# Attention over heads in a four-layer gated cross-attention stack: half-height products for the row maxima, and reciprocals by Ln, Exp and a Newton step

## The chip, the core and the metric

The kernel runs on one core of one Trainium2 chip. The metric is the device time of a whole run in microseconds; shown are the median and the ends of several runs. A profile comes from one further execution, and its span is counted from the first to the last recorded instruction.

The engines are called as the profile calls them: PE is TensorE's products, PEld its weight loads, DVE is VectorE, ACT is ScalarE, POOL is GpSimd, and SP is the queue that issues most DMAs.

## What is computed

A residual stream `x` of 2 batches x 1024 positions x 256 channels passes four layers. Each layer adds a gated cross-attention to a short context (77 rows per batch) and then a gated feed-forward block. Layers 0, 2 and 3 attend with 16 heads of 16 channels; layer 1 attends with one head over all 256 channels. Layer 2 turns queries and keys by position (rope). Layers 2 and 3 mask context rows. Cut to an attention over heads, the reference is:

```
q = heads(layernorm(x) @ Wq + bq)        # 16 heads, 16 channels each
k = heads(ctx @ Wk + bk);  v = heads(ctx @ Wv + bv)
s = q k^T * scale;  s = where(mask, -big, s)
p = softmax(s);  o = p v
x = x + tanh(g) * (o @ Wo + bo)
```

The feed-forward blocks are a mixture of 8 experts with a shared one, a mixture of 16, a quantised two-layer block, and a mixture of 8 with a shared one. The change leaves them alone.

## The kernel before

Everything is float32 unless it is a mask or a piece of a maximum. The 2048 rows of `x` stay in SBUF as 16 tiles of 128 rows, in four blocks `j` of four tiles `k`. `heads_attention` (lines 390 to 634) does layers 0, 2 and 3; it is a generator whose first part (keys, values and the tables made of them) can run under the feed-forward block before it.

**Its preparation.** `kT` holds the keys with channels on partitions, in two halves `ec` of 128 channels (8 heads each). `kbd` (line 430) repeats them 8 times along the free axis, each time kept for one head's 16 partitions only by `headmask`, so that one product of 128 partitions with four such groups gives four heads' scores side by side (4 x 77 = 308 columns). `kz` and `va` are the tables for the probabilities and for the values.

**Its loop.** For each block `j` these steps follow one another in an order written out in lines 611 to 629, which runs several blocks at once:

- `norm(j)`: layernorm of the rows, transposed to `hT`; the power -0.5 is on POOL.
- `queries(j, ec)`: the projection to `qT`.
- `maxima(j, k)`: for each `ec` and each half `hf` of the eight heads, one float32 product of 308 columns on all 128 partitions (line 498), in layers 2 and 3 a bfloat16 product that adds the mask (line 504), and a VectorE reduce that takes the maximum of each head's 77 scores, negated (line 508). Each result lies in one of four PSUM tiles of the pool `mm`, which nearly all products share in turn.
- `split(j)` and `turned(j)`: the maxima are split in three bfloat16 parts and transposed to `MT`.
- `probabilities(j, ec, i)`: the scores again, now with the context on partitions, as four products on quarters of the partitions (line 546); the maxima are subtracted by a product with a selection matrix (line 553), and ScalarE takes Exp (line 561).
- `combine(j, ec)`: sums `pz` and weighted values `pa` by two groups of products (line 574). VectorE takes the reciprocal of the sums (line 579) and multiplies (line 582), which gives `atT`.
- `finish(j)`: the output projection (line 589), added to `x` with the gate `tg` (line 593).

A block's `maxima` run between the `probabilities` of the block before it; the last block has none to run there. In layers 2 and 3, `behind` starts the norm of the following feed-forward block on finished rows. The framework that builds the program may move an instruction ahead of others on its engine where its inputs allow it, so the order on an engine can differ a little from the order of the code. It also puts in the loads of ScalarE's function tables where the next function is not in the loaded set.

Of the kernel before, what the change touches and what calls it, by code (L numbers as in the profile page):

```python
# [8 lines left out]
F32 = mybir.dt.float32  # L9
# [3 lines left out]
AF = mybir.ActivationFunctionType  # L13
ALU = mybir.AluOpType
AX = mybir.AxisListType
# [3 lines left out]
P = 128  # L19
D = 256  # L20
# [3 lines left out]
TB = 512  # L24
NK = 77
# [25 lines left out]
def flamingo_kernel(  # L51
# [4 lines left out]
    V, S, G, T = nc.vector, nc.scalar, nc.gpsimd, nc.tensor  # L56

    const = ctx.enter_context(tc.tile_pool(name="const", bufs=1))
# [11 lines left out]
    def mm(name, dt=F32, cols=512):  # L70
        return psA.tile([P, cols], dt, tag="mm", name=name)
# [5 lines left out]
    xs = []  # L77
# [60 lines left out]
    ident16 = const.tile([P, P], BF16, tag="ident16", name="ident16")  # L138
# [6 lines left out]
    headmask = const.tile([P, 8], F32, tag="headmask", name="headmask")  # L145
# [7 lines left out]
    )  # L153


    parity = const.tile([P, 2], F32, tag="parity", name="parity")
    for i in range(2):
        V.tensor_reduce(parity[:, i : i + 1], headmask[:, i::2], AX.X, ALU.add)
# [24 lines left out]

    tg = const.tile([P, 8], F32, tag="tg", name="tg")
    S.activation(tg, bc[:, 16:24], AF.Tanh)


    ctxT = const.tile([P, 2, 2 * NK], F32, tag="ctxT", name="ctxT")
# [7 lines left out]
    mskp = {}  # L196
# [115 lines left out]
    def bcl(ap, n):  # L312

        return ap.unsqueeze(2).to_broadcast([ap.shape[0], ap.shape[1], n])

    def bcm(ap, n):

        return ap.unsqueeze(1).to_broadcast([ap.shape[0], n, ap.shape[1]])
# [52 lines left out]
    def value(l, w, b):  # L371

        pv = mm(f"v{l}_{b}")
        for dc in range(2):
            T.matmul(
                pv[:NK, 0:D], lhsT=ctxT[:, dc, b * NK : (b + 1) * NK], rhs=w["v"][:, dc, :],
                start=(dc == 0), stop=(dc == 1),
            )
        return pv
# [10 lines left out]
    def heads_attention(l, ahead=None, behind=None):  # L390


        scale = 1.0 if l == 2 else 1.0 / 4.0
        with ExitStack() as st:
            ap1 = st.enter_context(tc.tile_pool(name=f"at1_{l}", bufs=1))
# [8 lines left out]
            kT = ap1.tile([P, 2, 2 * NK], F32, tag="kT", name=f"kT{l}")  # L404
# [22 lines left out]
                )  # L427
            kbd, vz = [], []
            for b in range(2):
                kb = ap1.tile([P, 2, 8, NK], F32, tag=f"kbd{b}", name=f"kbd{l}_{b}")  # L430
                for ec in range(2):
                    V.tensor_tensor(
                        kb[:, ec], bcm(kT[:, ec, b * NK : (b + 1) * NK], 8), bcl(headmask, NK), ALU.mult
                    )
                kbd.append(kb)
                va = ap1.tile([NK1, NH, 2 * DH], F32, tag=f"va{b}", name=f"va{l}_{b}")
                pv = value(l, w, b)
                G.memset(va, 0.0)
                for i in range(2):
                    V.tensor_tensor(  # L440
                        va[:NK, i::2, i * DH : (i + 1) * DH],
                        pv[:NK, 0:D].rearrange("p (h d) -> p h d", d=DH)[:, i::2, :],
                        w["bv"][:NK].rearrange("p (h d) -> p h d", d=DH)[:, i::2, :], ALU.add,
                    )
                vz.append(va)
# [12 lines left out]
            ap2 = st.enter_context(tc.tile_pool(name=f"at2_{l}", bufs=2))  # L458
            ap3 = st.enter_context(tc.tile_pool(name=f"at3_{l}", bufs=3))
            ap4 = st.enter_context(tc.tile_pool(name=f"at4_{l}", bufs=4))  # L460
            hTs, qTs, MTs, pTs, atTs, nms = {}, {}, {}, {}, {}, {}
# [27 lines left out]
            def maxima(j, k):  # L489

                i = 4 * j + k
                b, sq = i // NST, i % NST
                if k == 0:
                    nms[j] = ap2.tile([P, 4, 4, 2, 2], F32, tag="nm", name=f"nm{l}_{j}")
                for ec in range(2):
                    for hf in range(2):
                        ps = mm(f"sc{l}_{i}_{ec}_{hf}")
                        T.matmul(  # L498
                            ps[:, 0 : 4 * NK], lhsT=qTs[j][:, ec, k * P : (k + 1) * P],
                            rhs=kbd[b][:, ec, 4 * hf : 4 * hf + 4, :].rearrange("p h k -> p (h k)"),  # L500
                            start=True, stop=not masked,
                        )
                        if masked:
                            T.matmul(  # L504
                                ps[:, 0 : 4 * NK], lhsT=ident16, rhs=bcm(mskp[l][0][:, sq, :], 4),
                                start=False, stop=True,
                            )
                        V.tensor_reduce(  # L508
                            nms[j][:, k, 2 * hf : 2 * hf + 2, ec, :],
                            ps[:, 0 : 4 * NK].rearrange("p (r i k) -> p r i k", i=2, k=NK), AX.X, ALU.max, negate=True,  # L510
                        )

            def split(j):
# [17 lines left out]
            def turned(j):  # L531

                sq = (4 * j) % NST
                pm = mm(f"mT{l}_{j}", BF16, 1024)
                for k in range(4):
                    T.transpose(pm[:, k * P : (k + 1) * P], madd[:, sq + k, :], ident16)
                MTs[j] = ap2.tile([P, TB], BF16, tag="MT", name=f"MT{l}_{j}")
                S.copy(MTs[j], pm[:, 0:TB])

            def probabilities(j, ec, i):  # L540

# [22 lines left out]
            def combine(j, ec):  # L564

                b = j // 2
                nk = NK1 if l == 2 else NK
                pa, pz = mm(f"av{l}_{j}_{ec}"), mm(f"as{l}_{j}_{ec}")
                for po, lhsT in (
                    (pz, lambda r, i: ones2[:, i, :]), (pa, lambda r, i: vz[b][:, 8 * ec + 2 * r + i, :]),  # L570
                ):
                    for i in range(2):
                        for r in range(4):
                            T.matmul(  # L574
                                po[32 * r : 32 * r + 32, :], lhsT=lhsT(r, i)[:nk], rhs=pTs[j, ec, i][:nk, r, :],
                                start=(i == 0), stop=(i == 1),
                            )
                rz = ap1.tile([P, TB], F32, tag="rz", name=f"rz{l}_{j}_{ec}")
                V.reciprocal(rz, pz)  # L579
                if ec == 0:  # L580
                    atTs[j] = ap2.tile([P, 2, TB], F32, tag="atT", name=f"atT{l}_{j}")
                V.tensor_tensor(atTs[j][:, ec, :], pa, rz, ALU.mult)

            def finish(j):
                for k in range(4):
                    i = 4 * j + k
                    po = mm(f"o{l}_{i}")
                    for ec in range(2):
                        T.matmul(  # L589
                            po[:, 0:D], lhsT=atTs[j][:, ec, k * P : (k + 1) * P], rhs=w["o"][:, ec, :],  # L590
                            start=(ec == 0), stop=(ec == 1),
                        )
                    V.scalar_tensor_tensor(xs[i], po[:, 0:D], tg[:, l : l + 1], xs[i], ALU.mult, ALU.add)


            def has(step, j, *rest):
# [7 lines left out]
            for k in range(4):  # L604
                maxima(0, k)
# [1231 lines left out]
```

## Time and profile before

| | us |
|---|---|
| median of 3 runs | 1559.37 |
| lowest, highest | 1556.24, 1565.51 |
| profiled execution | 1588.63 |
| its span | 1586.9 |
| mean granted TensorE clock in it | 0.925 of full |

| group in the profile before | count | mean ns | busy us |
|---|---|---|---|
| L498 product for maxima (two records each) | 384 | 439 | 125.8 |
| L504 mask product | 128 | 304 | 38.9 |
| L508 maximum | 192 | 476 | 88.7 |
| L561 Exp | 96 | 1016 | 92.7 |
| L579 reciprocal | 24 | 3356 | 80.5 |
| L582 product with it | 24 | 692 | 16.6 |
| L432 `kbd` | 12 | 952 | 11.2 |

In a group's row of the profile, the numbers after the count are busy time and the mean duration of one; after the next bar stands the time for which the engine was idle just before these instructions, and what ended most of that. In the timeline a row gives the start, the time from the first start to the last end, the engine, the line, the operation, and how many instructions of that kind are merged. Product records overlap each other, so the distance between starts says more than a record's length.

### The profile page before, as it was taken

The page shows a single profiled execution, that of the slowest core. Times are in us where ns is not written, and L with a number is a line of the kernel's source. Part 1 is how long each engine was busy: PE and PEld are TensorE (multiplying, and loading weights), DVE is VectorE, ACT ScalarE, POOL GpSimd, SP SyncE. Part 2 cuts the span into 40 slices and gives each one's busy share as a digit, 9 for nine tenths or more (in the row PEclk, how much of TensorE's full clock was granted, in tenths as well). Part 3 has the DMA queues.
Part 4 walks back from the last instruction along what each step waited for, and adds up shares of the span by engine and source line. Part 5 has one row for each costly group of instructions (what it writes and reads, how often), then busy time and mean ns, then how long its engine had stood idle before and what let it go on. Part 6 is the DMA issues. An engine that isn't in the chain of part 4 may idle for free.

```text
span 1586.9 us, 18081 instructions
## 1 busy us (share of the span) xinstructions
PE 1358.2 (86%) x6798; PEld 901.4 (57%) x6800; DVE 890.0 (56%) x2168; ACT 403.7 (25%) x676; POOL 318.0 (20%) x367
## 2 busy tenths in 40 slices
PE   6999996999999999969759996889965899985783
PEld 3453445888888888536648883434433454344562
DVE  7676676444444444565653116757789667682124
ACT  1332430333333233213101111022355222211230
POOL 3200002222212110250010104400013400005661
PEclk9999997999999999989859997989987999997897
DMA  4001005565656556320315872000000000023545
GB/s 160 4 14 49 27 1 209 177 214 180 227 174 229 178 184 220 116 70 10 112 44 193 306 291 95 27 7 1 1 27 20 1 1 28 27 80 93 168 141 176
DMA packets 48362, 169.87 MB, mean 107 GB/s; under 512 B 9039, under 2 KB 27634, under 8 KB 42258
## 3 DMA queue, kind: packets, MB, share of 16 engines
q0 software_dynamic: 15600, 88.23, 16.0%
q1 hardware_dynamic: 25664, 74.33, 13.3%
q10 hardware_dynamic: 7010, 6.15, 1.3%
q8 instruction: 54, 0.88, 0.2%
q14 instruction: 34, 0.28, 0.1%
HBM read 147.97 MB, written 20.71 MB: 106 GB/s over the span
## 4 chain that ended last, share of the span: by engine, by line
PE 31%; DVE 11%; DMA 7%; issue 3%; POOL 2%; ACT 1%; another core or an unknown queue 1%; POOLq 0%; DVEq 0%; ACTq 0%; SPq 0%
DMA wbig<-in_wbig_dram 4%; PE sc L498 4%; PE q L384 2%; PE h L1199 2%; PE as L574 2%; PE gur L1557 2%; PE sT L546 2%; PE sT L553 2%; PE eo L1212 1%; PE av L574 1%; PE hs L941 1%; PE o L589 1%; PE gus L1557 1%; DVE hmax L1390 1%; PE eo_s L1007 1%
## 5 line engine op out<-in xcount | busy, mean ns | idle before, releaser
L941 PE MATMUL hr<-xgT0s,w 128*128 128x256 f32 (+1 forms) x1536 | 300.5, 346 | 11.5 <-DVE ulr L947 11.3
L941 PEld LDWEIGHTS hr<-xgT0s,w 128*128 128x128 f32 x1536 | 246.5, 191 | 55.6 <-DVE ulr L947 25.0
L561 ACT ACTIVATE pT<-sT 78x1024 f32<-78x1024 f32 x96 | 92.7, 1016 | 230.8 <-PE sT L553 208.9
L498 PE MATMUL sc<-kbd,qT 128*128 128x308 f32 x384 | 125.8, 439 | 7.3 <-DVE qT L480 6.2
L941 PE MATMUL hs<-hT_f,w0s 128*128 128x512 f32 x256 | 117.7, 602 | 5.5 <-DVE uls L947 2.2
L947 DVE SCALAR_TENSOR_TENSOR ulr<-hr,w,ulr 128x256 f32<-128x256 f32 (+1 forms) x96 | 41.6, 434 | 130.1 <-ACT ulr L946 129.5
L508 DVE TENSOR_REDUCE nm<-sc 128x4 f32<-128x308 f32 x192 | 88.7, 476 | 45.1 <-PE sc L504 33.4
L579 DVE RECIPROCAL rz<-as 128x512 f32<-128x512 f32 x24 | 80.5, 3356 | 29.6 <-PE as L574 29.6
L498 PEld LDWEIGHTS sc<-kbd,qT 128*128 128x128 f32 x384 | 68.3, 197 | 44.7 <-issue 19.6
L941 PEld LDWEIGHTS hs<-hT_f,w0s 128*128 128x128 f32 x256 | 46.9, 193 | 56.6 <-issue 47.9
L946 ACT ACTIVATE ulr<-hr,w 128x256 f32<-128x256 f32 (+1 forms) x96 | 41.7, 434 | 146.2 <-PE hr L941 146.0
L1025 PE MATMUL eo<-w,hid_r 128*128 128x256 f32 x312 | 77.5, 379 | 0.0
L384 PE MATMUL q<-hT_a,aw 128*128 128x512 f32 x128 | 71.5, 692 | 7.0 <-DVE hT_a L306 4.9
L1199 PE MATMUL h<-xgTs,wbig 128*128 128x128 f32 x512 | 62.7, 283 | 5.7 <-DMA wbig<-in_wbig_dram 5.7
L1199 PEld LDWEIGHTS h<-xgTs,wbig 128*128 128x128 f32 x512 | 61.1, 198 | 9.4 <-issue 6.0
L969 POOL DMA_INDIRECT w<-in_wbig_dram,r_wr_f x24 | 23.2, 965 | 212.7 <-PE hr L941 130.9
L1557 PE MATMUL gur<-xT3s,w 128*128 128x256 f32 (+1 forms) x192 | 50.0, 414 | 14.4 <-ACT xT3s L1605 7.8
L1549 DVE TENSOR_TENSOR sg_r<-gur,sg_r 128x256 f32<-128x256 f32 (+1 forms) x24 | 9.0, 375 | 94.9 <-ACT sg_r L1548 49.4
L1025 PEld LDWEIGHTS eo<-w,hid_r 128*128 128x128 f32 x312 | 57.8, 190 | 7.6 <-issue 0.5
L946 ACT ACTIVATE ugr<-hr,w 128x256 f32<-128x256 f32 (+1 forms) x96 | 41.7, 434 | 77.9 <-PE hr L941 71.1
L1212 PE MATMUL eo<-wbig,hh 128*128 128x256 f32 x256 | 59.9, 379 | 0.0
L947 DVE SCALAR_TENSOR_TENSOR ugr<-hr,w,ugr 128x256 f32<-128x256 f32 (+1 forms) x96 | 41.5, 433 | 31.4 <-ACT ugr L946 15.4
(457 smaller groups left out, 2295.1 us busy)
## 6 DMA issues: line engine op xcount, KB each, us to landing
wbig<-in_wbig_dram SPq DMA_DIRECT2D x17, 2048.0 KB
w<-in_wbig_dram SPq DMA_DIRECT2D x24, 384.0 KB
w0s<-in_wbig_dram SPq DMA_DIRECT2D x2, 2048.0 KB
h_dram<-h_f SPq DMA_DIRECT2D x32, 128.0 KB
y<-y_dram SPq DMA_DIRECT2D x4, 1024.0 KB
eo_dram<-eo0s SPq DMA_DIRECT2D x15, 256.0 KB
x<-in_x_dram SPq DMA_DIRECT2D x4, 512.0 KB
aw<-in_aw_dram SPq DMA_DIRECT2D x2, 1024.0 KB
```

The source lines that it names most:

```text
L384: T.matmul(pq, lhsT=w[m][:, dc, ec * P : (ec + 1) * P], rhs=hT[:, dc, :], start=(dc == 0), stop=(dc == 1),)
L498: T.matmul(ps[:, 0 : 4 * NK], lhsT=qTs[j][:, ec, k * P : (k + 1) * P], rhs=kbd[b][:, ec, 4 * hf : 4 * hf + 4, :].rearrange("p h k -> p (h ...
L508: V.tensor_reduce(nms[j][:, k, 2 * hf : 2 * hf + 2, ec, :], ps[:, 0 : 4 * NK].rearrange("p (r i k) -> p r i k", i=2, k=NK), AX.X, ALU.max, ...
L561: S.activation(pT[:, 2 * a : 2 * a + 2, :], pp[a][:NK1], AF.Exp, scale=scale)
L579: V.reciprocal(rz, pz)
L941: T.matmul(both[a][:, wi, :], lhsT=w13[:, dc, wi, a, ic * P : (ic + 1) * P], rhs=rhs(dc), start=(dc == 0), stop=(dc == 1),)
L946: S.activation(uu, both[a][:, 0, :], AF.Identity, bias=bias[:, 0, a, ic : ic + 1])
L947: V.scalar_tensor_tensor(uu, both[a][:, 1, :], bias[:, 1, a, ic : ic + 1], uu, ALU.add, ALU.mult)
L1025: T.matmul(po[:, s * D : (s + 1) * D], lhsT=hid[:, ic, s * P : (s + 1) * P], rhs=w2[:, ic, :], start=(ic == 0), stop=(ic == 3),)
L1199: T.matmul(ph[:, fc // 4, (fc % 4) * C : (fc % 4 + 1) * C], lhsT=w1[:, dc, fc * P : (fc + 1) * P], rhs=xgTs[e][:, dc, :], start=(dc == 0), ...
L1212: T.matmul(po[:, 0:D], lhsT=hs[e][:, fc // 4, (fc % 4) * C : (fc % 4 + 1) * C], rhs=w2[:, fc, :], start=(fc == 0), stop=(fc == NF - 1),)
L1557: T.matmul(pa[:, s, 0:n], lhsT=w[:, s, dc, :], rhs=rhs(dc), start=(dc == 0), stop=(dc == 1))
```

## The change

Three things change in `heads_attention`, and two small tables are made for them at the start.

**The products for the maxima.** `kbd` repeats the keys 4 times instead of 8, masked by `headmask4`, which is the sum of the two halves of `headmask`: column `h` keeps head `h` on partitions 0 to 63 and head `h + 4` on partitions 64 to 127. For each `ec`, the half `hf` now multiplies only partitions `64 hf` to `64 hf + 63` of `qT` and `kbd`, again with 308 columns. Both PSUM tiles are taken first, both float32 products follow one another, and then, in a second loop, come the mask products (as before, on all partitions) and the reduces.

**The reciprocal.** ScalarE takes Ln of the sums and Exp of its negative, which gives an approximate reciprocal `r`. VectorE computes `at = pa * r`, then `pz * r`, then `(pz * r - 2) * at`. This is a Newton step with its sign turned, so `finish` multiplies by `ntg`, the negated gate. `rz` now has two buffers.

**The table.** After the copy of `MT` for block 0, one load of ScalarE's table set that holds both Ln and Exp is issued.

```diff
+    headmask4 = const.tile([P, 4], F32, tag="headmask4", name="headmask4")
+    V.tensor_tensor(headmask4, headmask[:, 0:4], headmask[:, 4:8], ALU.add)
...
+    ntg = const.tile([P, 4], F32, tag="ntg", name="ntg")
+    V.tensor_scalar(ntg, tg[:, 0:4], -1.0, None, ALU.mult)
...
-                kb = ap1.tile([P, 2, 8, NK], F32, tag=f"kbd{b}", name=f"kbd{l}_{b}")
+                kb = ap1.tile([P, 2, 4, NK], F32, tag=f"kbd{b}", name=f"kbd{l}_{b}")
...
-                        kb[:, ec], bcm(kT[:, ec, b * NK : (b + 1) * NK], 8), bcl(headmask, NK), ALU.mult
+                        kb[:, ec], bcm(kT[:, ec, b * NK : (b + 1) * NK], 4), bcl(headmask4, NK), ALU.mult
...
+                    ps = [mm(f"sc{l}_{i}_{ec}_{hf}") for hf in range(2)]
                     for hf in range(2):
-                        ps = mm(f"sc{l}_{i}_{ec}_{hf}")
+                        half = slice(64 * hf, 64 * hf + 64)
                         T.matmul(
-                            ps[:, 0 : 4 * NK], lhsT=qTs[j][:, ec, k * P : (k + 1) * P],
-                            rhs=kbd[b][:, ec, 4 * hf : 4 * hf + 4, :].rearrange("p h k -> p (h k)"),
+                            ps[hf][:, 0 : 4 * NK], lhsT=qTs[j][half, ec, k * P : (k + 1) * P],
+                            rhs=kbd[b][half, ec].rearrange("p h k -> p (h k)"),
                             start=True, stop=not masked,
                         )
+                    for hf in range(2):
                         if masked:
                             T.matmul(
-                                ps[:, 0 : 4 * NK], lhsT=ident16, rhs=bcm(mskp[l][0][:, sq, :], 4),
+                                ps[hf][:, 0 : 4 * NK], lhsT=ident16, rhs=bcm(mskp[l][0][:, sq, :], 4),
...
-                S.copy(MTs[j], pm[:, 0:TB])
+                copied = S.copy(MTs[j], pm[:, 0:TB])
+                if j == 0:
+                    with tc.issue_after(copied.ins):
+                        S.preload_act_table_set("natural_log_exp_and_others")
...
-                rz = ap1.tile([P, TB], F32, tag="rz", name=f"rz{l}_{j}_{ec}")
-                V.reciprocal(rz, pz)
+                rz = ap2.tile([P, TB], F32, tag="rz", name=f"rz{l}_{j}_{ec}")
+                S.activation(rz, pz, AF.Ln)
+                S.activation(rz, rz, AF.Exp, scale=-1.0)
...
-                V.tensor_tensor(atTs[j][:, ec, :], pa, rz, ALU.mult)
+                at = atTs[j][:, ec, :]
+                V.tensor_tensor(at, pa, rz, ALU.mult)
+                V.tensor_tensor(rz, pz, rz, ALU.mult)
+                V.scalar_tensor_tensor(at, rz, 2.0, at, ALU.subtract, ALU.mult)
...
-                    V.scalar_tensor_tensor(xs[i], po[:, 0:D], tg[:, l : l + 1], xs[i], ALU.mult, ALU.add)
+                    V.scalar_tensor_tensor(xs[i], po[:, 0:D], ntg[:, l : l + 1], xs[i], ALU.mult, ALU.add)
```

## The prediction

> **What bounds the kernel now.** First the page: its busy rows and the slices that hold the three attentions over heads (slices 1 to 4, 26 to 30 and 32 to 35 of 40).
>
> ```profile
> span 1586.9 us, 18081 instructions
> PE 1358.2 (86%) x6798; PEld 901.4 (57%) x6800; DVE 890.0 (56%) x2168; ACT 403.7 (25%) x676; POOL 318.0 (20%) x367
> PE   6999996999999999969759996889965899985783
> DVE  7676676444444444565653116757789667682124
> ```
>
> Then the stage windows of the three loops, in layers 0, 2 and 3 (columns: window, length, busy PE, PEld, DVE, ACT, POOL, granted clock, DMA).
>
> ```profile
> 60.00:119.00 59.00, 58.09 (x360) 29.16 (x362) 44.19 (x85) 20.49 (x24) 2.03 (x2) 1.00 0.03 10
> 1060.00:1123.00 63.00, 60.91 (x344) 30.54 (x344) 45.90 (x91) 13.99 (x15) 2.03 (x2) 1.00 0.00 1
> 1236.00:1347.00 111.00, 110.57 (x592) 55.39 (x592) 75.05 (x169) 30.50 (x37) 14.38 (x18) 0.98 0.03 10
> ```
>
> TensorE is occupied 97 to 100% of the loops at full clock and nothing waits long on DMA; VectorE has a quarter to a third free, ScalarE two thirds. A microsecond of TensorE work removed there is a microsecond of time, unless VectorE is late behind it. Then the groups that the change touches:
>
> ```profile
> L498 PE MATMUL sc<-kbd,qT 128*128 128x308 f32 x384 | 125.8, 439 | 7.3 <-DVE qT L480 6.2
> L508 DVE TENSOR_REDUCE nm<-sc 128x4 f32<-128x308 f32 x192 | 88.7, 476 | 45.1 <-PE sc L504 33.4
> L579 DVE RECIPROCAL rz<-as 128x512 f32<-128x512 f32 x24 | 80.5, 3356 | 29.6 <-PE as L574 29.6
> L432 DVE TENSOR_TENSOR kbd<-kT,headmask 128x616 f32<-128x616 f32 x12 | 11.2, 952 | 0.0
> ```
>
> A float32 product is two matmul records (384 for 192). Records overlap, so I price by distance between starts, from the timeline:
>
> ```profile
> 79.90 4.31 PE L498 MATMUL sc<-kbd,qT 128*128 128x308 f32 x16
> 84.04 0.38 PE L589 MATMUL o<-aw,atT 128*128 128x256 f32 x1
> 1299.09 0.30 PE L504 MATMUL sc<-madd,ident 128*128 128x308 bf16 x1
> 1299.75 0.30 PE L504 MATMUL sc<-madd,ident 128*128 128x308 bf16 x1
> ```
>
> Layer 0: eight products in 4.14 us, 0.517 each. Layers 2 and 3: 0.655 per product with its mask; so the mask is 0.655-0.517, about 0.13. A pair of half-head groups (one `i`, one `ec`) costs 1.035 without and 1.31 with masks.
>
> **The pairs.** The new operands lie on partitions 0-63 and 64-127. Whether such products run together, L546 shows; it already uses quarters of the partitions:
>
> ```profile
> 1337.81 0.67 PE L546 MATMUL sT<-qT,kz 32*78 32x512 f32 x4
> 1338.30 0.61 PE L546 MATMUL sT<-qT,kz 32*78 32x512 f32 x4
> 1338.84 0.41 PE L553 MATMUL sT<-MT,pick 128*78 128x512 bf16 x1
> ```
>
> Four first passes start together, four second passes 0.49 later, the next, full-height product 0.54 after those. A pass of 512 columns is 0.43 (L384 spaces its weight loads so), so eight passes took 1.03 us where a queue of them would take 3.41. The excess over 0.86 is 0.06 for the first weights (78 columns) and 0.1 for emptying the array where the height changes.
>
> So a new pair is 0.517. In layer 0 neighbours have one height: 1.035 becomes 0.517. In layers 2 and 3 each pair goes to half height and back for its masks: weights 0.11 (0.06 scaled to 128 columns) + 0.517 + change 0.1 + first mask weights 0.03 + masks 0.26 + change 0.1 = 1.11, a saving of 0.20. The Trainium skill speaks against this part: "TensorEngine Tiling (Array Packing)", Key Properties, says that a change of tiling mode drains TensorE. It gives no price; the row's 0.1 is used. Taken as free, 64 masked pairs would save 26 us; with it, 12.8.
>
> What of it reaches the end:
> - Layer 0, three turns of the loop. Reduces of L508 run back to back at 0.41 us (four in 1.63 at 91.56), and four PSUM tiles turn under all `mm` products. For k=0 and k=3, four tiles: 2.07 becomes 1.03, saving 1.0 each. For k=1 and 2 together, the fifth tile waits for a reduce: 4.14 becomes about 2.75, saving 1.4. 3 x 3.4 = 10.2. But k=3 meets a busy VectorE at 91.56: `as` already waited 0.91 for it; that 1.0 and some of the next goes into the wait. Kept: 8. The opening `maxima(0)` (29 to 37 us) runs at VectorE's pace: nothing.
> - Layers 2 and 3: k=0 saves 0.4, k=1,2 0.8, k=3 0.4 only where no norm of finished rows stands ahead of its reduces (one turn of three; `as` already waits 1.04, 1.05, 0.38 and 0.38 in the others). 3 x 1.2 + 0.4 = 4 each, and 1 each in the openings: 10.
>
> **Smaller `kbd`.** L432 halves to 308 elements: twelve instructions from 0.95 to about 0.55 (L425, 308 elements, 0.61). In layer 0 four of them (3.3 us) stand ahead of the copy of `hT` that TensorE awaits at 21.63: 1.5, less 0.1 for the new `headmask4`. In layer 3 they lie in the VectorE-bound stage (1206 to 1211, 4.7 us): 2.1. Layer 2 prepares them under other work: 0. Sum 3.5. If covers existed there too, 0.
>
> **The reciprocal.** Out: 3.36 on VectorE, 24 times. In: on ScalarE Ln (PSUM, 512 columns: L1205, 0.60) and Exp (SBUF: L953, 0.63); on VectorE two more operations of 0.69 (L582, L956). From sums to `atT`: before 3.36 + 0.10 + 0.69 = 4.15; after 0.60 + 0.63 + 3 x 0.69 + 0.1 for hand-overs = 3.4. Inside the loop this lies under the next products, and nothing follows but freedom: VectorE gets 24 x (3.36 - 1.38) = 47 us back, ScalarE gives 30, 1.2 per combine, out of its idle two thirds. On the path it lies twice per layer, at the last turn without maxima to cover it:
>
> ```profile
> 1353.71 3.36 DVE L579 RECIPROCAL rz<-as 128x512 f32<-128x512 f32 x1 [4.77 <-PE as L574]
> 1357.17 0.69 DVE L582 TENSOR_TENSOR atT<-av,rz 128x512 f32<-128x512 f32 x1
> 1357.92 2.24 PEld L589 LDWEIGHTS o<-aw,atT 128*128 128x128 f32 x11 [0.50 <-DVE atT L582]
> ```
>
> 6 x 0.75 = 4.5. New waits: Ln waits on ScalarE for the sums, with the next Exps behind it; these need a product of L553 that ends over 3 us later (sums done 1364.9, next Exp 1368.47), so they lose nothing. VectorE's product waits 1.3 us for Exp; queued behind it are reduces and `hT` copies that before waited 3.36 for the reciprocal. The sums' tile is held 0.60+0.63+1.38, not 3.36, so PSUM comes free earlier.
>
> **The table.** One preload per head layer behind a copy; the row of L953's loads says 1.28 us. The Trainium skill, "ScalarE: Activation LUTs", What ACT_TABLE_LOAD costs, says 2.66 with its drain. At most three: 3.8 or 8.0 us of ScalarE, which is idle there 1 us or more; the path gets 0.1 each by the row, 1.4 by the page. I take 0.3 in all. Should the loads alternate between Ln and Exp, see below. `ntg` is nothing.
>
> **Sum:** 8 + 10 + 1.4 + 2.1 + 4.5 - 0.3 = 25.7 off the profiled 1586.9 (1588.6 with its surroundings). That execution is 29 above the median; its head stages run at full clock, so the same microseconds are taken from 1559.4: **1533.7**, 1.6%.
>
> **Rivals.**
> (1) As summed, 1534; own range 1521 to 1546, as VectorE eats half of the layer 0 and masked gain, or none. Chance 0.65.
> (2) VectorE sets the pace: each burst of pairs ends in a wait for its reduce, and the maxima give a third (6). 1559.4 - 6 - 7.7 = 1546, at worst 1555. For it: `as` waits on `nm` now. Against: VectorE loses 50 us of work in these stages. Chance 0.14.
> (3) Slower: halves do not run side by side. Masked pairs then cost 1.035 + 0.6 = 1.63, 64 x 0.32 = 20 more; layer 0 nothing; minus 7.7: 1571. It decides when a pair takes over about 0.9 instead of 0.517 (26 us fall by 66 per us added). Against: L546. For: no half-height product is in this trace. Chance 0.10.
> (4) Tables alternate, two loads per combine: 48 x 1.28 = 61 us of ScalarE, most hidden, 3 us in each of six exposed chains: 1534 + 18 = 1552. Against: Tanh and Exp share one load before. Chance 0.05.
> (5) VectorE's freedom also shortens the openings and the norm waits: 1515. Chance 0.06. (The order of instructions on an engine is not the code's, e.g. `as` at 1348.24 ahead of `sT`; a new order can add a few us to any case.)
>
> **The numbers.** A measurement here tells 0.5%, 7.8 us. Faster by that: nearly all of (1) and (5), two thirds of (2): 0.80; same: the rest of (2), (4) and an edge of (3): 0.11; slower: (3): 0.09. Range 1514 to 1558: it leaves out (3) and the ends of (2), (4) and (5).
>
> **What would show it.** Products of 64 rows starting in twos, half of the loops' L498 spacing in layer 0, and about 1.1 us per masked pair; Ln before Exp with at most three new table loads; no L579; `as` waits on `nm` up by 1 to 2 us per turn. The prediction is wrong if 64-row products start one after another, if a change of height costs over 0.2, or if a table load stands at each combine.

## The result and the profile after

The changed kernel takes 1547.49 us (median of 7 runs, 1544.84 to 1552.55) where the kernel before takes 1559.72 beside it; the ratio is 0.9922, 95% interval 0.9905 to 0.9939. That is 12.2 us less (9.5 to 14.8), where 25.7 were forecast. Of the profiled execution the span is 1548.9 us.

First the page of the changed kernel: busy rows, and the slices of TensorE and VectorE.

```profile
span 1548.9 us, 18125 instructions
PE 1337.7 (86%) x6798; PEld 861.6 (56%) x6800; DVE 831.7 (54%) x2194; ACT 437.6 (28%) x727; POOL 316.0 (20%) x367
...
PE   5999987999999999969849996889977799996873
...
DVE  7565675444444444466562115755569945566214
```

VectorE lost 58 us of work (the forecast: 47 from the reciprocals and about 5 from `kbd`) and ScalarE gained 34, as worked out. The slices say little; the stage windows say more (window, length, busy PE, PEld, DVE, ACT, POOL, granted clock, DMA). The first, second and last row are the loops of layers 0, 2 and 3; the third and fourth row lie inside layer 2's loop.

```profile
55.00:110.00 55.00, 52.63 (x368) 23.41 (x364) 34.64 (x89) 23.74 (x30) 1.02 (x1) 1.00 0.03 11
1060.00:1123.00 63.00, 60.07 (x314) 22.16 (x316) 33.15 (x83) 18.14 (x22) 2.02 (x2) 0.84 0.00 1
1069.60:1080.00 10.40, 10.38 (x45) 2.61 (x46) 4.46 (x12) 1.92 (x3) 0.00 (x0) 0.52 0.00 0
1107.00:1118.00 11.00, 10.73 (x48) 2.81 (x48) 4.71 (x13) 2.16 (x4) 0.00 (x0) 0.53 0.01 1
1219.00:1330.00 111.00, 106.00 (x598) 42.48 (x600) 67.87 (x187) 38.03 (x48) 18.14 (x22) 0.97 0.03 10
```

Before, layer 2's loop ran at a granted clock of 1.00. Now it has 0.84, and the two inner rows show why: twice, for some 10 us, TensorE is busy all the time at half its clock. Busy time alone hides this; only the clock column tells.

The groups that the change touches:

```profile
L505 PE MATMUL sc<-kbd,qT 64*128 64x308 f32 x384 | 83.0, 501 | 5.7 <-DVE qT L485 3.5 <-DVE nm L516 1.1 <-ACT qT L492 1.1
L516 DVE TENSOR_REDUCE nm<-sc 128x4 f32<-128x308 f32 x192 | 81.2, 470 | 44.3 <-PE sc L512 32.6 <-PE sc L505 11.3
L597 DVE TENSOR_TENSOR atT<-av,rz 128x512 f32<-128x512 f32 x24 | 16.6, 692 | 75.1 <-PE av L586 75.1
L592 ACT ACTIVATE rz<-as 128x512 f32<-128x512 f32 x24 | 14.3, 597 | 45.7 <-PE as L586 45.6
L437 DVE TENSOR_TENSOR kbd<-kT,headmask 128x308 f32<-128x308 f32 x12 | 7.3, 629 | 0.0
L550 ACT ACT_TABLE_LOAD x3 | 3.8, 1283 | 0.1
```

The products for the maxima have 64 rows now; the tables cost three loads in all. `L597` is the product `pa * rz`: where VectorE stands idle in front of it, 75.1 us in all, it waits for the values `av`, never for the reciprocal.

The timeline of the changed kernel (start, time from first start to last end, engine, line, how many, idle time before) in layer 0 and, after the first dots, around the first wait in layer 2:

```profile
84.13 1.31 PE L505 MATMUL sc<-kbd,qT 64*128 64x308 f32 x8
...
87.38 1.92 PE L586 MATMUL as<-pT,ones 77*32 77x512 f32 x16 [1.94 <-DVE nm L516]
...
1065.89 0.79 PE L505 MATMUL sc<-kbd,qT 64*128 64x308 f32 x4
1066.54 1.38 DVE L1327 TENSOR_SCALAR h<-x,mv_f,rs_f 128x256 f32<-128x256 f32 x4 [1.20 <-POOL rs_f L1325]
...
1066.61 0.45 PE L512 MATMUL sc<-madd,ident 128*128 128x308 bf16 x2
1066.99 0.79 PE L505 MATMUL sc<-kbd,qT 64*128 64x308 f32 x4
...
1067.96 1.22 DVE L1330 TENSOR_REDUCE rmax<-h 128x4 f32<-128x1024 f32 x1
1069.10 1.62 DVE L516 TENSOR_REDUCE nm<-sc 128x4 f32<-128x308 f32 x4
1069.62 3.29 PE L586 MATMUL as<-pT,ones 78*32 78x512 f32 x16 [1.46 <-DVE nm L516]
...
1072.67 3.66 PE L586 MATMUL av<-pT,va 78*32 78x512 f32 x16
```

Eight records, two pairs, take 1.31 us in layer 0 from the first start to the last end; two products start together each time, and the later starts in that row are 0.26 apart, two of them to a pair, so 0.52 a pair. A masked pair takes 1066.99 - 1065.89 = 1.10: 0.72 to its first mask product and 0.38 from there to the next pair, where the forecast had 0.73 and 0.39. So halves run side by side, at the forecast prices (0.517 and 1.11). Then VectorE, which has the four scalings `h` and the reduce `rmax` of the next block's norm ahead of the four reduces of k=3, lets TensorE wait 1.46 us. The sums `as` that follow take 3.29 us, where layer 0's take 1.92: the half clock has begun. In the kernel before, the same place has a shorter wait and sums at full speed:

```profile
1083.96 1.38 DVE L1310 TENSOR_SCALAR h<-x,mv_f,rs_f 128x256 f32<-128x256 f32 x4 [1.20 <-POOL rs_f L1308]
1085.38 1.22 DVE L1313 TENSOR_REDUCE rmax<-h 128x4 f32<-128x1024 f32 x1
...
1085.70 0.30 PE L504 MATMUL sc<-madd,ident 128*128 128x308 bf16 x1
1087.04 1.92 PE L574 MATMUL as<-pT,ones 78*32 78x512 f32 x16 [1.04 <-DVE nm L508]
```

Chips differ: the kernel before lies at 1557.8 to 1587 us on those used below, mostly because the last feed-forward block, from its first to its last Sigmoid, takes 139 to 144 us in some profiles and 162 to 167 in others, with and without the change. So whole runs are compared by their ratio to the kernel before on the same chip, and traces by stage. The three attentions over heads, from the first Exp of a layer to the end of its last `finish`, in us, with the waits on VectorE above 0.5 us in the loops of layers 0 and 2 and the half-speed stretches behind them:

| kernel | ratio to before [95%] | layer 0 | layer 2 | layer 3 | waits (us), half speed behind them (us) |
|---|---|---|---|---|---|
| before, shown profile | 1 | 105.6 | 137.9 | 117.8 | 0.91, 0.68; 1.04, 1.05: none |
| changed | 0.9922 [0.9905, 0.9939] | 98.3 | 142.5 | 112.1 | 1.94; 1.46, 1.47: 0; 10.2, 10.2 |
| before_again | 1.0015 [0.9996, 1.0034] | 105.7 | 137.5 | 117.8 | as before: none |
| before_rmax_twice | 1.0052 [1.0033, 1.0072] | 105.4 | 143.2 | 117.8 | 0.91, 0.67; 2.17, 2.17: 0, 0; 0, 6.8 |
| late_rmax | 0.9869 [0.9847, 0.9891] | 98.1 | 130.2 | 112.1 | 1.95; no other: none |
| newton_first | 0.9921 [0.9892, 0.9950] | 102.9 | 137.2 | 112.2 | 1.94; 1.47, 1.47: 10.2; 0, 10.2 |
| after_again | 0.9935 [0.9912, 0.9959] | 101.3 | 136.2 | 112.1 | 1.95; 1.47, 1.47: 6.8; 0, 6.8 |
| masked_full | 0.9937 [0.9915, 0.9960] | 104.3 | 135.7 | 116.6 | 1.95; 1.04, 1.05: 10.2; none |
| combined | 0.9843 [0.9822, 0.9865] | 103.9 | 130.5 | 112.1 | 1.95; no other: 10.2 |
| best | 0.9820 [0.9801, 0.9838] | 97.3 | 130.0 | 112.1 | none above 0.5 |
| pairs_only | 0.9925 [0.9904, 0.9945] | 105.0 | 137.5 | 113.5 | 1.94, 0.68; 1.46, 1.47: 10.2, 0; 0, 6.8 |
| recip_only | 0.9983 [0.9973, 0.9993] | 104.2 | 136.1 | 116.6 | 0.91; 1.05, 1.04: none |
| late_both | 0.9847 [0.9823, 0.9871] | 96.4 | 129.5 | 112.1 | none above 0.5 |
| pairs_late | 0.9895 [0.9865, 0.9924] | 99.6 | 135.9 | 113.5 | 1.35, 0.67; 1.68, 1.68: 0, 0; 0, 3.4 |

In layers 0 and 3 the profile of the changed kernel is shorter, by 7.3 and 5.7; in layer 2 it is longer by 4.6.

### The profile page after: what moved, and what is told of

Read it like the earlier page. It is cut to its first block, busy times and chain, and to the rows that moved or that the text cites. A ratio compares the mean times of both kernels' runs of the same rounds, so it can differ in the third digit from the quotient of the medians.

```text
span 1548.9 us, 18125 instructions
## 1 busy us (share of the span) xinstructions
PE 1337.7 (86%) x6798; PEld 861.6 (56%) x6800; DVE 831.7 (54%) x2194; ACT 437.6 (28%) x727; POOL 316.0 (20%) x367
## 4 chain that ended last, share of the span: by engine, by line
PE 32%; DVE 12%; DMA 7%; POOL 3%; issue 2%; ACT 1%; POOLq 0%; ACTq 0%; DVEq 0%; SPq 0%
DMA wbig<-in_wbig_dram 4%; PE h L1216 3%; PE as L586 2%; PE q L389 2%; PE sc L505 2%; PE sT L558 2%; PE av L586 2%; PE gur L1574 2%; PE sT L565 2%; PE eo L1229 2%; PE hs L958 1%; PE o L606 1%; PE sc L512 1%; PE gus L1574 1%; DMA y_dram<-eo3s,dest 1%
## 5 line engine op out<-in xcount | busy, mean ns | idle before, releaser
L516 DVE TENSOR_REDUCE nm<-sc 128x4 f32<-128x308 f32 x192 | 81.2, 470 | 44.3 <-PE sc L512 32.6
L505 PE MATMUL sc<-kbd,qT 64*128 64x308 f32 x384 | 83.0, 501 | 5.7 <-DVE qT L485 3.5
L558 PE MATMUL sT<-qT,kz 32*78 32x512 f32 x384 | 61.3, 657 | 0.0
L505 PEld LDWEIGHTS sc<-kbd,qT 64*128 64x128 f32 x384 | 37.4, 198 | 40.7 <-issue 16.6
L586 PE MATMUL as<-pT,ones 77*32 77x512 f32 (+1 forms) x384 | 54.8, 631 | 5.6 <-DVE nm L516 5.3
L597 DVE TENSOR_TENSOR atT<-av,rz 128x512 f32<-128x512 f32 x24 | 16.6, 692 | 75.1 <-PE av L586 75.1
```

Source lines behind the costliest of these rows:

```text
L505: T.matmul(ps[hf][:, 0 : 4 * NK], lhsT=qTs[j][half, ec, k * P : (k + 1) * P], rhs=kbd[b][half, ec].rearrange("p h k -> p (h k)"), start=Tr ...
L516: V.tensor_reduce(nms[j][:, k, 2 * hf : 2 * hf + 2, ec, :], ps[hf][:, 0 : 4 * NK].rearrange("p (r i k) -> p r i k", i=2, k=NK), AX.X, ALU. ...
L558: T.matmul(pp[r // 2][:NK1, r % 2, :], lhsT=kz[rows_, i, ec, b, :], rhs=qTs[j][rows_, ec, :], start=True, stop=False,)
L586: T.matmul(po[32 * r : 32 * r + 32, :], lhsT=lhsT(r, i)[:nk], rhs=pTs[j, ec, i][:nk, r, :], start=(i == 0), stop=(i == 1),)
```

## The experiments

**The half clock in layer 2.** The theory: the change lengthened two waits on VectorE, and these cost not only their own length but a stretch at half clock each. The rival: layer 2 lost its gain to VectorE's pace or to dearer masked pairs, and the clock fell by accident. The first run moves one VectorE instruction, `rmax`, behind the reduces for which TensorE waits; nothing else is edited.

```diff
-    mskp = {}
+    mskp, marks = {}, {}
...
-                        V.tensor_reduce(
+                        marks["max"] = V.tensor_reduce(
                             nms[j][:, k, 2 * hf : 2 * hf + 2, ec, :],
...
-        V.tensor_reduce(q2["max"][:, blk], h2[:, blk, :], AX.X, ALU.max)
+        with tc.issue_after(marks["max"].ins):
+            V.tensor_reduce(q2["max"][:, blk], h2[:, blk, :], AX.X, ALU.max)
```

> The changed kernel; only the 1.22 us maximum over the normalised rows (norm2's last instruction) is issued behind the last reduce of the maxima that stand ready, so that those reduces start 1.2 us earlier and the sums' product waits about 0.2 to 0.3 us in place of 1.46. Theory A (the 1.46 us wait makes TensorE's clock halve for 10.2 us, twice): no half-speed stretch in layer 2's loop, 10 to 12 us less than the changed kernel, near 1536. Theory C (layer 2 loses by the changes of height and by the queue for PSUM): only the two waits go, 2 to 3 us less, near 1545.

The timeline at the same place of this kernel, and the window that holds its loop in layer 2:

```profile
1073.40 1.38 DVE L1327 TENSOR_SCALAR h<-x,mv_f,rs_f 128x256 f32<-128x256 f32 x4 [1.20 <-POOL rs_f L1325]
...
1074.70 1.63 DVE L516 TENSOR_REDUCE nm<-sc 128x4 f32<-128x308 f32 x4
1075.23 1.92 PE L586 MATMUL as<-pT,ones 78*32 78x512 f32 x16 [0.21 <-DVE nm L516]
1076.24 1.22 DVE L1331 TENSOR_REDUCE rmax<-h 128x4 f32<-128x1024 f32 x1
...
1060.00:1123.00 63.00, 62.57 (x370) 25.34 (x369) 39.73 (x95) 22.11 (x27) 2.02 (x2) 1.00 0.00 1
```

The wait falls from 1.46 to 0.21, the clock is 1.00, and layer 2 takes 130.2 us instead of 142.5. The 12.3 us are accounted for: two waits shorter by 1.25 (2.5) and 20.4 us no longer at half clock (10.2), together 12.7. The ratio falls from 0.992 to 0.987, which is about 8 us; the first expectation had named 10 to 12, the second 2 to 3.

The second run goes the other way: the kernel before with a second, unused reduce of the size of `rmax` ahead of the first.

```diff
+        q2["spare"] = w2p.tile([P, NTI], F32, tag="rmax2", name="rmax2")
...
+        V.tensor_reduce(q2["spare"][:, blk], h2[:, blk, :], AX.X, ALU.max)
         V.tensor_reduce(q2["max"][:, blk], h2[:, blk, :], AX.X, ALU.max)
```

> The kernel before with one more reduce of 1.22 us over the normalised rows in each block's norm2, whose result nobody reads, so that the sums' product waits about 2.2 us in place of 1.04 in layer 2. Theory A: the clock halves there as in the changed kernel, without any half-height product in the program: two or more half-speed stretches of 10 us in layer 2's loop and 10 to 14 us more than before, 1570 to 1574. Theory C: only the reduces' own time, 3 to 5 us more, 1563 to 1565.

Its timeline at the second of the two waits, and the window behind it:

```profile
1119.85 2.38 PE L574 MATMUL as<-pT,ones 78*32 78x512 f32 x16 [2.17 <-DVE nm L508]
1121.98 3.66 PE L574 MATMUL av<-pT,va 78*32 78x512 f32 x16
...
1121.20:1128.00 6.80, 6.80 (x34) 1.41 (x27) 5.01 (x8) 0.00 (x0) 0.00 (x0) 0.50 0.01 2
```

Both waits are 2.17 us; only the second is followed by half speed, for 6.8 us. Layer 2 takes 5.5 us more than the kernel before has on average: 2 x 1.12 of longer wait and 3.4 for the stretch. The ratio, 1.0052 or 8 us, lies between the two expectations, for one stretch of 6.8 us came and not two of 10. So the effect can be made without the change, but a wait does not bring it every time. The kernel before by itself, run beside these, is the scale for such differences.

> The kernel before, unchanged, for a second trace of it. Theory A (the changed kernel loses in layer 2 because TensorE's granted clock halves there): no half-speed stretch inside layer 2's loop (first to last finish), as in the first trace, and the stage from the last row of layer 2's feed-forward Relu group's end to the last finish of layer 2 again near 203 us. Theory B (such half-speed stretches fall into layer 2's loop by chance in either kernel): one or more of them here. The last stage, which took 161 us from its first to its last Sigmoid in the first trace and 141 in the changed kernel's, tells whether that difference is chance: then it is nearer to 141 here.

It gave 1.0015, no half speed in the loops, and layers within 0.4 us of the first profile.

Next, whether the changed kernel does it again:

> The changed kernel unaltered, a second profile. Theory A (the two half-speed stretches belong to the two VectorE waits of 1.4 to 1.5 us in layer 2's loop): the waits are there again, at least one of the two is followed by a half-speed stretch of 10.2 us, layer 2's stage takes 202 to 208 us (197 to 198 without a stretch, 5 us for each), the ratio to the kernel before is 0.990 to 0.994. Rival B (the stretches were an accident of one execution, unrelated to the waits): waits of 1.47 us and no half-speed stretch in layer 2, stage near 197 us, ratio 0.986 or below.

Its timeline in layer 2, at the first and at the second wait:

```profile
1072.64 1.92 PE L586 MATMUL as<-pT,ones 78*32 78x512 f32 x16 [1.47 <-DVE nm L516]
...
1105.31 2.35 PE L586 MATMUL as<-pT,ones 78*32 78x512 f32 x16 [1.47 <-DVE nm L516]
1107.41 3.66 PE L586 MATMUL av<-pT,va 78*32 78x512 f32 x16
```

The waits are the same; this time only the second is followed by half speed, for 6.8 us, and layer 0's wait of 1.95 is too. Layer 2 is 6.0 us above `late_rmax`: 2.5 for waits and 3.4 for the stretch. The theory held in that at least one of the two was followed, but the stretch was 6.8 us and not 10.2; what layer 2 loses differs from execution to execution, 3.4 us here and 10.2 in the first profile. Layer 2's stage, 203.1 us from the last Relu ahead of it, lies in the range named.

**What the masked pairs are worth.** The products of layers 2 and 3 at full height again, the rest as changed:

```diff
+                nh, hm = (8, headmask) if l in mskp else (4, headmask4)
...
+                if masked:
...
+                            T.matmul(
+                                ps[:, 0 : 4 * NK], lhsT=qTs[j][:, ec, k * P : (k + 1) * P],
+                                rhs=kbd[b][:, ec, 4 * hf : 4 * hf + 4, :].rearrange("p h k -> p (h k)"),
+                                start=True, stop=not masked,
+                            )
...
+                else:
...
-                rz = ap2.tile([P, TB], F32, tag="rz", name=f"rz{l}_{j}_{ec}")
+                rz = (ap1 if masked else ap2).tile([P, TB], F32, tag="rz", name=f"rz{l}_{j}_{ec}")
```

> The changed kernel with the products for the maxima of the masked layers 2 and 3 at full height, one after the other, as before the change (kbd with 8 heads there; rz with one buffer there for want of room). By the prediction's sum (masked pairs worth 5 us in each of the two layers, and the pad of kbd 2.1 in layer 3): layer 2 takes 212 us, layer 3 182, ratio 0.999 to 1.000. Theory A (shorter pairs made the waits longer, and these brought the half speed): waits in layer 2's loop back at 1.0 to 1.1 us, no half-speed stretch, so layer 2 takes 202 to 203 us (207 + 5 - 10), layer 3 182, ratio 0.994 to 0.997: in layer 2 the pairs cost 4 to 5 us net.

Its timeline at the first wait of layer 2, and the window:

```profile
1075.38 1.92 PE L606 MATMUL as<-pT,ones 78*32 78x512 f32 x16 [1.04 <-DVE nm L515]
...
1060.00:1123.00 63.00, 60.91 (x355) 28.85 (x353) 38.37 (x92) 19.35 (x24) 2.02 (x2) 1.00 0.00 1
```

The waits are back at 1.04 and 1.05, and the half clock is gone from layer 2: 135.7 us, against 136.2 and 142.5 in the two profiles of the changed kernel. With `rmax` out of the way the pairs give 130.2; of these 5.5 us less, 1.7 are shorter waits, which leaves 3.8 for the pairs (forecast 4). In the changed kernel's order they lose all of it in one profile, and 6.8 us besides in the other. In layer 3, where no wait stands, they give 116.6 - 112.1 = 4.5. The whole time is no worse than the changed kernel's (0.9937 against 0.9935 beside it).

**The two parts alone.** The pairs and the narrower `kbd` without the edits of the reciprocal and the table (`pairs_only`), and the reverse (`recip_only`: full-height products, `kbd` with 8 heads, `rz` with one buffer). Against the changed kernel the first is:

```diff
...
-                copied = S.copy(MTs[j], pm[:, 0:TB])
-                if j == 0:
-                    with tc.issue_after(copied.ins):
-                        S.preload_act_table_set("natural_log_exp_and_others")
+                S.copy(MTs[j], pm[:, 0:TB])
...
-                rz = ap2.tile([P, TB], F32, tag="rz", name=f"rz{l}_{j}_{ec}")
-                S.activation(rz, pz, AF.Ln)
-                S.activation(rz, rz, AF.Exp, scale=-1.0)
+                rz = ap1.tile([P, TB], F32, tag="rz", name=f"rz{l}_{j}_{ec}")
+                V.reciprocal(rz, pz)
...
-                V.tensor_tensor(at, pa, rz, ALU.mult)
-                V.tensor_tensor(rz, pz, rz, ALU.mult)
-                V.scalar_tensor_tensor(at, rz, 2.0, at, ALU.subtract, ALU.mult)
+                V.tensor_tensor(atTs[j][:, ec, :], pa, rz, ALU.mult)
...
```

> The kernel before with the half-height pairs and the narrower kbd alone; VectorE keeps its 24 reciprocals of 3.36 us. If the two parts of the change simply add up: layer 0 about 1 us above the changed kernel's 144.4 without half speed (two tails of some 0.2, and Ln/Exp not there), layer 3 near 214 for the stretch from layer 2's end to its own (221.4 before), ratio 0.990 to 0.994. If the reciprocals stand in the way (each is 2.1 us longer on VectorE than the two products that replace it, ahead of the reduces that TensorE waits for): waits of more than 2 us in the loops of layers 0 and 2, half-speed stretches behind some of them, layer 0 at 147 to 153, layer 2's stretch at 206 to 212 (203.1 before), ratio 0.995 to 1.002.

> The kernel before with the reciprocals by logarithm, exponential and Newton step alone (table preload and negated gate with it; one buffer for rz); the products for the maxima stay at full height, one after the other. By the tails as measured (0.2 each, six of them) minus 1 us, and the waits of 0.9 to 1.05 us in the loops at most gone (4 of them): minus 1 to minus 5 us, ratio 0.997 to 0.999, no half-speed stretch in a loop. Rival (the freed VectorE time of some 58 us is worth more than the waits seen): below 0.996. Rival on the other side (the added Ln and Exp delay ScalarE's copies and exponentials): above 1.000.

The pairs alone give 0.9925, as much as the whole change. Their waits are those of the changed kernel to 0.01 us (1.94, 1.46, 1.47), so it is the pairs that lengthen them, by ending earlier, and not the new reciprocal. The stages came out at the "in the way" end in layer 0, by half speed, and the ratio at the other: neither expectation fits whole. The reciprocal alone gives 0.9983, 2.7 us, with no half speed, as expected.

**The order of the Newton step.** In the changed kernel, the product with the values comes first and waits for `av`. The other order refines `rz` while `av` runs:

```diff
-                V.tensor_tensor(at, pa, rz, ALU.mult)
-                V.tensor_tensor(rz, pz, rz, ALU.mult)
-                V.scalar_tensor_tensor(at, rz, 2.0, at, ALU.subtract, ALU.mult)
+                V.tensor_tensor(at, pz, rz, ALU.mult)
+                V.scalar_tensor_tensor(rz, at, 2.0, rz, ALU.subtract, ALU.mult)
+                V.tensor_tensor(at, pa, rz, ALU.mult)
```

> The changed kernel; the Newton step is made on the reciprocal before the weighted values are multiplied in, with the same three VectorE operations. Theory D (the chain from sums to the result was 3.9 us because its first VectorE operation waits for the weighted values, which end 1.75 us after the sums): two of the three operations run under that wait, one 0.69 us operation is left behind the weighted values, the chain is about 3.0 us, and six exposed chains give 4 us: 1543 to 1544. Against it (another thing ends last in the tail): under 1 us.

No gain that shows: the ratio is 0.9921, but its interval of 0.6% could not tell a gain of 4 us. The traces can. The chain from the sums to `atT` at a layer's end does fall from 3.93 to 3.50 us, but the output products that follow fall into another order, and from the start of Ln to the end of the layer it is 6.69 us instead of 6.50, in each of the three layers. A shorter chain into TensorE was not a shorter layer.

**Without the waits.** Two further versions take waits away by order alone. `combined` has `rmax` late and the other Newton order. `best` has, besides, the first scaling of the norm that stands ahead of k=3 in layer 0 issued behind those reduces:

```diff
...
         for k in range(4):
             h = lnp.tile([P, D], F32, tag="h", name=f"h_{tagp}_{j}_{k}", bufs=4)
-            V.tensor_scalar(
-                h, xs[4 * j + k], mv[:, k, 0:1], rs[:, k : k + 1], ALU.subtract, ALU.mult
-            )
+            with ExitStack() as late:
+                if tagp == "f0" and k == 0:
+                    late.enter_context(tc.issue_after(marks[0, min(j + 2, 3)].ins))
+                V.tensor_scalar(
+                    h, xs[4 * j + k], mv[:, k, 0:1], rs[:, k : k + 1], ALU.subtract, ALU.mult
+                )
...
```

> The changed kernel with rmax of norm2 issued behind the last reduce of k = 3, and the Newton step made on the reciprocal before the product with the values (three products as before, other order). Theory: no half-speed stretch in layer 2's loop, its stage 197 us (198.6 with rmax alone, less two tails of 0.7); layer 3 174 us (175.5 less 1.4); layer 0 143 us if the wait of 1.94 us is not followed by half speed, 148 if it is. Ratio 0.982 to 0.986, faster than the changed kernel (0.992) and than rmax alone (0.987). Rival (the tail is bound by the products that follow it, not by the chain): stages as with rmax alone, ratio 0.987.

> As the run before, and in addition the first of the four scalings of ffn0's first norm (h_f, 1.3 us of VectorE ahead of the last reduces of k = 3 in layer 0) issued behind those reduces. Theory: layer 0's wait of 1.94 us falls to 0.6 or less, its stage to 141.5 to 142 us with no half speed in it, ratio 0.980 to 0.984, never above the run before. Rival (the wait only moves, to the transposes of h_f or to the gate products that need it): layer 0's stage stays at 143 or grows, ratio as in the run before or 0.001 above.

`combined` met half speed for 10.2 us behind layer 0's wait, as its expectation left open, and still gave 0.9843. In `best` that wait is gone. Its timeline in layer 0, and the window of layer 2's loop:

```profile
85.40 1.63 DVE L519 TENSOR_REDUCE nm<-sc 128x4 f32<-128x308 f32 x4 [0.59 <-PE sc L508]
85.93 1.92 PE L589 MATMUL as<-pT,ones 77*32 77x512 f32 x16
86.95 0.40 DVE L307 TENSOR_SCALAR h_f<-x,mv_f,rs_f 128x256 f32<-128x256 f32 x1
...
1052.00:1115.00 63.00, 62.58 (x382) 26.05 (x382) 40.88 (x105) 21.86 (x27) 2.65 (x3) 1.00 0.00 1
```

The reduces run before the scalings, the sums `as` do not wait at all. The median is 1531.52 us (1529.21 to 1532.32) beside 1557.76 for the kernel before and 1548.01 for the changed one: it beats both.

Last, the same two moves with the changed kernel's own Newton order, and with the reciprocals back on VectorE:

> The changed kernel with both instructions issued behind the reduces of k = 3 (rmax of norm2 in layer 2, the first scaling h_f of ffn0's first norm in layer 0), the Newton step in the changed kernel's own order. If the waits are the whole of what was lost: no wait above 0.5 us and no half speed in the loops of layers 0 and 2, ratio 0.980 to 0.984 as in the run with the other order too, which then is worth nothing (its chain from the sums to atT is 3.50 instead of 3.93 us, but the output products after it end 0.2 later). If the other order was worth the 0.4 us per tail that the chain shows: 0.002 above that run, 0.984 or more.

> The pairs and the narrower kbd alone (VectorE keeps its 24 reciprocals), with the same two instructions issued behind the reduces of k = 3. Theory (the reciprocal part is worth its ends of layers: 0.84 us in layers 0 and 2, 0.2 in layer 3, 0.2 at the third turn of each, 2.6 in all): no wait above 0.7 us in the loops, no half speed, ratio 0.0017 above the run beside it, 0.982 to 0.986. Rival (VectorE with its reciprocals is too late for the pairs once they stand closer): waits above 1 us remain and half speed returns, ratio 0.988 or more; the reciprocal part is then needed for the pairs.

`late_both` gave 0.9847, on another chip than `best` (0.9820). By the ratio alone this is where the expectation puts it if the other order counts; but the intervals overlap, and its layers 0 and 2 are 0.9 and 0.5 us shorter than those of `best`, so the other Newton order is not needed. `pairs_late` gave 0.9895, 0.0048 above the run beside it: waits and half speed came back as the rival said. Its timeline in layer 2 shows a reciprocal in the middle of the split of the maxima:

```profile
1067.48 1.21 DVE L1323 TENSOR_REDUCE rmax<-h 128x4 f32<-128x1024 f32 x1
1068.61 0.21 DVE L527 TENSOR_TENSOR nm<-nm,left 128x64 f32<-128x64 f32 x1
1068.74 3.35 DVE L588 RECIPROCAL rz<-as 128x512 f32<-128x512 f32 x1
1072.01 0.13 DVE L536 CAST maddt<-nm 128x64 bf16<-128x64 f32 x1
...
1073.80 0.40 PE L545 MATMUL mT<-ident,maddt 128*128 128x128 bf16 x4 [1.68 <-DVE maddt L536]
```

One instruction of 3.35 us stands between the maxima and their transposes, and TensorE waits 1.68. So the reciprocal's part, worth 2.7 us alone and nothing that shows beside the pairs in the given order, is worth more once the other waits are gone: in these two profiles layers 0, 2 and 3 are 3.2, 6.4 and 1.4 us longer without it, and half speed is 1.7 of the 6.4. By the whole runs the size is less sure: the ratios differ by 0.0048, 7.6 us, the medians by 5.4, and the two intervals just overlap.

## Why the prediction was right or wrong

**Right: the prices.** Halves run side by side (0.517 and 1.10 per pair, forecast 0.517 and 1.11). The 12 `kbd` instructions fell to 0.63 (forecast 0.55), and layer 0's first query product started at 20.52 instead of 21.63 (forecast 1.4 earlier). Three table loads of 1.283, none per combine, and no wait that names them; where a next instruction stands ready, at two of the three, it starts 1.31 us after the copy ahead of the load ends, so the row's price held and not the 2.66 of the page that the prediction named. Rivals 3 and 4 are out. The drain that the Trainium skill names for a change of tiling mode ("TensorEngine Tiling (Array Packing)", Key Properties) fits into the 1.10 at the 0.1 taken from the row; how the 0.32 us beyond the products and masks divide into drain and weights is not shown.

**Near by luck: the sum, for a loop without waits.** `late_both` is the change with two instructions moved. Against the kernel before, the end of layer 0 came at 142.2 instead of 153.2 (forecast 10.9 earlier), layer 2's loop takes 129.5 instead of 137.7 (mean of two; forecast 6.5 less), and from layer 2's end to layer 3's it is 214.3 instead of 221.4 (forecast 8.6 less). Together 11.0 + 8.2 + 7.1 = 26.3, forecast 25.7. The whole runs show 24.2 (20.4 to 28.1) there and 28.0 (25.2 to 31.0) in `best`. But the two moved instructions also take away waits of 0.91, 1.04 and 1.05 us that the kernel before had and that the forecast did not count as gain; about 0.2 is left of each in layer 2 and nothing in layer 0, which makes 2.6 us. The change as given, with the half speed of its two profiles taken off, gains 21.5 and 22.1 us in these three places. So the terms add up to some 4 us too much, and the agreement to half a microsecond is luck.

**Wrong: a wait priced by its own length, with TensorE at full clock.** The step that failed reads: "a microsecond of TensorE work removed there is a microsecond of time, unless VectorE is late behind it", and for k=3 a saving "only where no norm of finished rows stands ahead of its reduces". It took a longer wait to cost, at worst, what the shorter pairs saved, and put the clock behind it at nothing. The waits did grow, by 0.4 us each in layer 2 and from 0.91 to 1.94 in layer 0, less than the "1 to 2 us per turn" that the prediction named. But behind a wait of that length TensorE can lose half its clock for 3.4 to 10.2 us, which costs 1.7 to 5.1 us. In the two profiles of the changed kernel this cost 10.2 and 6.8 us. In layer 2 it took 10.2 us in the first, more than the whole gain forecast there (142.5, where 137.7 less 6.5 was expected), and 3.4 in the second (136.2). Of the shortfall of 13.5 us in the median, it explains about 7 to 10. Of the 4 us that remain, 1.3 are the reciprocal's term (below); the growth of the waits is no more than what the forecast had let go at k=3, and what the other 2 to 3 us are is not shown. The signs were in the profile before: the waits of 1.04 and 1.05, with 2.6 us of `h` and `rmax` ahead of the awaited reduces in VectorE's queue. What that profile could not show is the price.

**The rivals.** Rival 2 (VectorE sets the pace) named 1546, near the result, and rightly the wait on the reduces; but the maxima gave more than its third (the end of layer 0 came 8.8 us earlier of the 10.9 forecast, layer 3 was 7.3 shorter of 8.6), and when the waits went the rest came. The time agrees, the mechanism only in part.

**The reciprocal's term.** Forecast 4.5, twice 0.75 in each layer. Alone it gave 2.7 (1.1 to 4.2), and the loops in that run are shorter by 1.4, 1.6 and 1.2. The end of a layer, from the start of the reciprocal or of Ln to the last `finish`, went from 7.34 to 6.50 in all three layers, which is 0.84 for the forecast's 0.75. That this is near is luck too: the chain to `atT`, from which the 0.75 was worked out, fell there from 4.15 to 3.93 alone, and the other 0.6 came behind it, in the output products and the last additions to `x`. At the other of the two places the term was too large. The lines of the changed kernel that answer to those shown of before, at layer 3's third turn:

```profile
1337.15 0.60 ACT L592 ACTIVATE rz<-as 128x512 f32<-128x512 f32 x1 [0.37 <-PE as L586]
1337.78 0.63 ACT L593 ACTIVATE rz<-rz 128x512 f32<-128x512 f32 x1
...
1338.94 0.69 DVE L597 TENSOR_TENSOR atT<-av,rz 128x512 f32<-128x512 f32 x1 [7.09 <-PE av L586]
...
1340.39 0.69 DVE L599 SCALAR_TENSOR_TENSOR atT<-rz,atT 128x512 f32<-128x512 f32 x1
...
1341.13 2.89 PEld L606 LDWEIGHTS o<-aw,atT 128*128 128x128 f32 x14 [0.28 <-DVE atT L599]
```

From the sums to the weights it is 3.98 us, 4.21 before: 0.23. Together that is 1.07 per layer for 1.5, so 3.2 us for 4.5. The forecast let the first VectorE product follow Exp at once, at 1338.41; it waits until 1338.94 for `av`.

## What to carry over

A wait of TensorE between products is not priced by its own length: where a change shortens the work in front of a wait that another engine ends, read the clock column of the windows behind it, and ask which instructions stand ahead of the awaited ones without need. Here moving one reduce of 1.2 us and one scaling behind the reduces that TensorE awaits about doubled the gain of this change. A part of a change that is worth little beside the rest may be worth more once another wait is gone; so test the parts again after the bottleneck has moved.

## What was not expected of the hardware

Half speed came after waits much shorter than the stretches that it lasted. Over the 14 profiles, in layer 0's loop from 55 us on and in the last 95 us of layer 2, a wait of TensorE of 1.34 to 2.17 us, whatever ended it, was followed within 2.2 us by a half-speed stretch 12 times of 22; a wait of 0.67 to 1.05 us within the loops never, 17 times. In these windows no stretch came without such a wait. At a place just ahead of them, at 53 to 55 us, TensorE waits for ScalarE's `qT`: 1.41 to 1.72 us there brought 3.4 us of half speed three times of six (`best` is one of the three), 1.05 to 1.17 never in four. The same wait of 1.94 or 1.95 us at the same place in layer 0 brought half speed in five profiles of seven, at starts that differ by under 1.5 us.

Most of this chance has an order, found in the same profiles afterwards and not tested by a run of its own. The stretches are multiples of 3.413 us (3.4, 6.8, 10.2), and within one profile all their starts lie on one grid of that step, to 0.002 us: in the changed kernel, 1070.03 and 1107.58 us are 11 steps apart. Of the 28 waits of 1.34 to 2.17 us above, those that began in the first 1.64 us of a step were followed by half speed 13 times of 14, those that began 1.86 to 2.80 us into it once of 13; the last began at 3.32, just ahead of the next step, and was followed. So what looked like chance is in good part the place in the step at which a wait begins. What sets the length of a stretch stays open.

The Trainium skill, "TensorE: Matmul & The Clock Gate", Part 1, tells of a free-running activity window of 3413 ns, which fits this grid. Its section "Why this matters for your kernels" says that gaps above some 3 us are to be avoided; here gaps of 1.46 and 1.47 us were enough, five times of eight, so the measurement decides. What was not tried is how the window weighs the products just before the wait: in layers 0 and 2 a burst of products for the maxima always stands there, so a wait of 1.5 us elsewhere may be harmless.
